# Loading and combining layer 0's weights differently at the start of a four-layer graph network kernel

## The chip, the cores and the metric

The kernel runs on one NeuronCore of a Trainium2 chip. A core has five engines, each with its own in-order queue: TensorE (PE; its weight loads are shown apart as PEld), VectorE (DVE), ScalarE (ACT), GpSimd (POOL) and SyncE (SP), which here only issues DMAs. ACT issues some DMAs too. All arithmetic is float32. The metric is the device time of one execution in microseconds (us); lower is better.

## The reference, cut to what matters

Four graph layers run one after another on x of 128 graphs x 128 nodes x 512 features. The change concerns layer 0 alone:

```python
Xw = X @ Wv + bv
sj = Xw @ aw[:d, 0]
si = Xw @ aw[d:, 0]
e = jax.nn.leaky_relu(sj[:, None, :] + si[:, :, None] + ab[0], negative_slope=0.2)
alpha_matrix = A * jnp.exp(e)
transition = alpha_matrix / (jnp.sum(alpha_matrix, axis=-1, keepdims=True) + 1e-12)
for k in range(Wk.shape[0]):          # K = 3
    H = H + Xk @ Wk[k] + bk[k]
    Xk = jnp.einsum('bij,bjd->bid', transition, Xk)
x = _layernorm(x + relu(H))
```

`Wv` is 512x512, `Wk` 3x512x512, `aw` 1024x1. The kernel never forms `Xw`: the scores need only the two vectors `Wv @ aw[:d]` and `Wv @ aw[d:]`, and it appends these as two more columns to the three `Wk` matrices.

## The kernel before

**Planner.** The kernel doesn't issue instructions as its Python runs. Each call on an engine is recorded in a `Plan` (line 173) with a due value (`plan.key`), an estimated cost and the tiles that it touches. `order` (238) then places all of them by list scheduling, on each engine the ready operation of the lowest due value or latest deadline first, takes tiles out of small pools (12 and later more buffers of kind `four`, 8 of `sq`, 6 PSUM banks and two more, `t0` and `t1`), and `emit` (364) issues them in that order. All instructions thus carry line 375 in the profile, and groups are told apart by their tiles. DMAs rotate through eight completion semaphores, called lanes here: a DMA is issued only when the DMA that last used its lane has landed, whichever of SP and ACT issued that.

**Products.** Every large product uses Strassen's scheme in Winograd's form, with seven block products in place of eight. In layer 0 it is applied twice (`twice`, 830, over `strassen`, 618): seven outer weights B11, B21, T2, T1, B22, T3, N4, and each of these holds seven inner blocks of 128 x 386 (three matrices' 128 columns each, and the two score columns). T1 = B12 - B11, T3 = B22 - B12, T2 = B22 - T1, N4 = B21 - T2. A 128x386 product is one matmul instruction and two records in the profile. The left operands are sums and differences of transposed x, made by POOL in `lefts` (793).

**Setup.** `prepare0` (882) makes the weights. `Wk` comes in four quarters: chunk pair g (0 or 1) by column half (0 or 1); a quarter and a matrix m is one `fetch` (898), four DMAs of 32 partitions each, 64 KB apiece. The two quarters of the left column half are issued from ACT (`fetch_quarter(ac, ...)`, 910 and 911), the two of the right half from SP (922, 923). They land in `stage`, three of the seven outer weight tiles (`first` in the profile). ACT copies each into place: twelve copies `first<-first 128x512`. Two `fetch` calls bring `Wv` (128 KB a DMA). `aw` is loaded broadcast over 128 partitions (`awb`), and eight `dot` calls (477) multiply rows of `Wv` with it and sum (DVE `junk<-four,four`), which gives the score columns. `combine` (503) makes the inner T3, T1, T2 and N4 of one quarter: three ACT copies into PSUM and four DVE subtractions. When B12 and B22 are there, `combine_once_more` (509) makes the outer weights: for each of seven inner blocks two ACT copies into `t0` and `t1` and two DVE subtractions (outer T1 and T2), and then two subtractions on POOL over whole tiles (`first<-first 128x2702`), outer T3 and N4. B12 is stored where T1 comes to lie.

**Two pairs of graphs.** `layer0` (967) takes four graphs at a time, transposes x (DVE `four<-four 128x1024`), makes the operands on POOL, runs the 49 block products, whose results DVE and ACT take out of the banks (`out<-bank`), and lets POOL add two `out` tiles (`out<-out 128x772`) after T1 and T3 (843 to 845). Then come attention, a round trip of the transition matrix through DRAM (`e`, `sq`), two more products into `t0` and `t1`, and the normalisation.

Of the kernel before, what the change touches and what calls it, by code (L numbers as in the profile page):

```python
# [14 lines left out]
OP = mybir.AluOpType  # L15
AX = mybir.AxisListType

P = 128
D = 512
C = D // P  # L20
# [34 lines left out]
B11, B21, T1, B22, T2, T3, N4 = range(7)  # L55
B12 = T1
# [9 lines left out]
QW = 3 * P + 2  # L66
# [311 lines left out]
def rows(ap, n):  # L378

    return bass.AP(tensor=ap.tensor, offset=ap.offset, ap=[[0, P], [1, n]])  # L380
# [3 lines left out]
def kernel(  # L384
# [20 lines left out]
    at = lambda kind, k: spans[kind][1] + k * SIZE[kind]  # L405
# [29 lines left out]
    for kind, k, t in (*(("out", k, t) for k, t in enumerate(outs)), ("w28", 0, places["w28"][0]),  # L435
                       ("row1", 0, row1)):
        for c in range(SIZE[kind] // SIZE["four"]):
            later["four", len(places["four"])] = [(kind, k)]
            places["four"].append(t[:, c * SIZE["four"]:(c + 1) * SIZE["four"]])
    plan = Plan(slots, later)  # L440
    pe, ve, ac, po, sp = (plan.engine(*e) for e in ((PE, nc.tensor), (DVE, nc.vector), (ACT, nc.scalar),
                                                     (POOL, nc.gpsimd), (SP, nc.sync)))

    def tile_of(kind, *shape, place=None):
        n = math.prod(shape)
        flat = View(Tile(kind, place=place), np.arange(SIZE[kind]))[:, :n]
        names = [f"a{k}" for k in range(len(shape))]
        return flat if len(shape) == 1 else flat.rearrange(
            f"p ({' '.join(names)}) -> p {' '.join(names)}", **dict(zip(names, shape)))

    def fixed(*shape, name, kind="fixed"):
        t = const.tile([P, *shape], FP, name=name)
        return View(Tile(kind, t), np.arange(math.prod(shape)).reshape(shape))

    def bank():
        return tile_of("bank", D)

    def four():

        return tile_of("four", U, D)  # L460
# [16 lines left out]
    def dot(dst, u, v, n=D):  # L477
        ve.scalar_tensor_tensor(junk[:, :n], u, 1.0, v, op0=OP.mult, op1=OP.mult, accum_out=dst)

    def row():  # L480
        return tile_of("row", D)
# [15 lines left out]
    def held_in_bank(kind, block):  # L497

        p = tile_of(kind, QW)
        ac.copy(p, block)  # L500
        return p

    def combine(W):

        c12, c22, c21 = (held_in_bank(k, W[:, j, 0]) for k, j in (("t0", B12), ("t1", B22), ("bank", B21)))
        for to, a, b in ((T3, c22, B12), (T1, c12, B11), (T2, c22, T1), (N4, c21, T2)):
            ve.tensor_tensor(W[:, to, 0], a, W[:, b, 0], OP.subtract)

    def combine_once_more(W):

        base = plan.key
        for n, i in enumerate((B11, T1, T2, B21, T3, B22, N4)):
            plan.key = base + .1 * n
            c12, c22 = (held_in_bank(k, W[j][:, i, 0]) for k, j in (("t0", B12), ("t1", B22)))
            for to, a, b in ((T1, c12, B11), (T2, c22, T1)):
                ve.tensor_tensor(W[to][:, i, 0], a, W[b][:, i, 0], OP.subtract)
        flat = [w.rearrange("p j o f -> p (j o f)") for w in W]
        for to, a, b in ((T3, T2, B11), (N4, B21, T2)):
            po.tensor_tensor(flat[to], flat[a], flat[b], OP.subtract)

    def prep():

# [358 lines left out]

    def prepare0():
        h = D // 2
        plan.key = -9.6
        awc, bvc = fixed(2 * C, name="aw_c"), fixed(C, name="bv_c")
        for c, v, n in ((awc, aw, 2 * C), (bvc, bv0, C)):
            sp.dma_start(c, bass.AP(tensor=v.tensor, offset=v.offset, ap=[[1, P], [P, n]]), run=1)
        ab_b, bk0b = fixed(1, name="ab_b"), row()
        sp.dma_start(bk0b[:3], bk0)
        sp.dma_start(ab_b, rows(ab, 1), run=1)  # L890
        plan.key = -9
        awb = four()
        sp.dma_start(awb.rearrange("p u f -> p (u f)"), rows(aw, 2 * D))
        W = WT["0"] = [tile_of("w7", 7, 1, QW, place=(B11, B21, T2, T1, B22, T3, N4).index(k)) for k in range(7)]
        stage = [W[T2 + m].rearrange("p j o f -> p (j o f)")[:, :C * D].rearrange("p (c f) -> p c f", f=D)
                 for m in range(3)]

        def fetch(queue, dst, src, chunks, columns, run):
            with plan.together():
                for k in range(4):  # L900
                    queue.dma_start(dst[k * Q:(k + 1) * Q],
                                    src.rearrange("(k c a) f -> k a c f", k=4, a=Q)[k][:, chunks, columns],
                                    run=run, parts=Q)

        def fetch_quarter(queue, g, half):
            for m in range(3):
                at = slice(2 * g, 2 * g + 2), slice(half * h, half * h + h)
                fetch(queue, stage[m][:, at[0], at[1]], wk0[m], *at, h)

        fetch_quarter(ac, 0, 0)  # L910
        fetch_quarter(ac, 1, 0)
        st = [four() for _ in range(2)]
        for g in range(2):
            fetch(sp, st[g], wv0, slice(2 * g, 2 * g + 2), slice(0, D), D)
        ones = fixed(P, name="ones")
        po.memset(ones, 1.0)
        two = fixed(C, 2, name="cols0")
        for c in range(C):
            for k in range(2):
                dot(two[:, c, k:k + 1], st[c // 2][:, c % 2], awb[:, k])  # L920
        plan.key = WHEN0[0] + .05
        fetch_quarter(sp, 0, 1)
        fetch_quarter(sp, 1, 1)
        plan.key = -9
        for g, half, j in ((0, 0, B11), (1, 0, B21), (0, 1, B12), (1, 1, B22)):
            for m in range(3):
                ac.copy(W[j][:, :4, :, m * P:(m + 1) * P].rearrange("p (n c) o i -> p c n (o i)", n=2),
                        stage[m].rearrange("p c (n i) -> p c n i", i=P)[:, 2 * g:2 * g + 2, 2 * half:2 * half + 2])
            scores = W[j][:, :4, 0, 3 * P:]
            if half:  # L930
                po.memset(scores, 0.0)
            else:
                po.memset(scores[:, 2:], 0.0)
                ac.copy(scores[:, :2], two[:, 2 * g:2 * g + 2])
            plan.key = COMBINE[half][g]
            combine(W[j])
            plan.key = -9
        plan.key = COMBINE[2]
        combine_once_more(W)
        plan.key = -9  # L940
        p = bank()
        aws = fixed(C, name="aw_sum")
        ve.tensor_add(aws, awc[:, :C], awc[:, C:])
        with plan.together(120):
            for j in range(C):
                pe.matmul(p[:, :1], aws[:, j:j + 1].to_broadcast([P, P]), bvc[:, j:j + 1],
                          start=j == 0, stop=j == C - 1)
        ve.tensor_tensor(c0, p[:, :1], ab_b, OP.add)

        p = bank()  # L950
        pe.matmul(p, ones[:3], bk0b[:3], start=True, stop=True)
        p = p.rearrange("p (h n i) -> p h n i", h=2, n=2)
        ac.copy(bias[:, 0], p[:, 0])
        ve.tensor_tensor(bias[:, 1], p[:, 1], bias[:, 0], OP.subtract)
        plan.key = WHENT[0][0] - .1
        for kind in ("t0", "t1"):
            p = tile_of(kind, D)
            pe.matmul(p, ones[:3], bk0b[:3], start=True, stop=True)
# [306 lines left out]
    h = D // 2  # L1265
# [246 lines left out]
    n = B // U  # L1512
# [18 lines left out]

    plan.key = -9
    prepare0()
    layer(layer0, 0, WHEN0, size=2)
    plan.late = LATE
# [38 lines left out]
```

## Time and profile before

| what | value |
|---|---|
| median of 3 runs | 5422.08 us (5418.66 to 5425.36) |
| the profiled execution | 5419.12 us, of which the span of the trace is 5417.3 us (1.8 us lie around it) |
| busy share of the span | PE 98%, PEld 78%, DVE 81%, ACT 44%, POOL 72% |
| mean granted TensorE clock | 0.998 |
| DMA | 814 MB, mean 150 GB/s |
| chain that ended last | PE 89%, DVE 4%, DMA 3%, waits for issue 2% |

Share by engine says what is busy on average. The chain that ended last follows the work back from the last instruction; a share of 89% for PE means that for most of the time an instruction on TensorE was what the end waited for. An engine's idle time in a stretch, and what is named as ending it, tells where that isn't so. Matmul ends are modelled, so a stretch in which PE reads as fully busy can hold idle time: in the first 10 us, for instance, PE reads 10.00 us busy with ten records, the last of which begins before 8 us.

### The profile page before, as it was taken

What the parts mean: (1) busy time and instruction counts of PE and PEld (TensorE: products, weight loads), DVE (VectorE), ACT (ScalarE), POOL (GpSimd) and SP (SyncE); (2) the same over time, 40 slices, a digit from 0 to 9 for tenths busy, and PEclk for the clock granted to TensorE, in tenths of its full rate; (3) what the DMA queues carried; (4) which work ended last, traced back from release to release, by engine and by line L of the source; (5) the groups of instructions that cost most, each with busy time, mean ns of one, the idle gap of its engine ahead of it and who ended that gap; (6) DMA issues with size and microseconds to landing.
All of it is one profiled execution on the core that took longest, in us unless ns stands there. A gap on an engine that the chain in (4) does not pass through costs nothing.

```text
span 5417.3 us, 93854 instructions
## 1 busy us (share of the span) xinstructions
PE 5318.2 (98%) x29035; PEld 4235.9 (78%) x29035; DVE 4411.2 (81%) x11725; ACT 2389.6 (44%) x6088; POOL 3907.2 (72%) x4931
## 2 busy tenths in 40 slices
PE   7999999999999999999999999999999999999998
PEld 3555555555788888888888888989988998999987
DVE  6778888887888888888888778778877877787886
ACT  3434334334444444444444444444444444444444
POOL 5777678765766666666767577778777777787776
PEclk9999999999999999999999999999999999999999
DMA  3444444445554545454545745545554555455543
GB/s 105 133 135 131 128 135 148 124 123 162 158 163 145 157 146 161 145 157 149 157 142 154 245 133 155 163 150 166 156 159 150 162 159 158 152 163 162 155 155 110
DMA packets 842748, 814.24 MB, mean 150 GB/s; under 512 B 269819, under 2 KB 643075, under 8 KB 842246
## 3 DMA queue, kind: packets, MB, share of 16 engines
q1 hardware_dynamic: 840326, 806.66, 48.5%
q8 instruction: 231, 3.78, 0.3%
q14 instruction: 271, 2.22, 0.1%
q10 hardware_dynamic: 1920, 1.57, 0.1%
HBM read 458.90 MB, written 349.04 MB: 149 GB/s over the span
## 4 chain that ended last, share of the span: by engine, by line
PE 89%; DVE 4%; DMA 3%; issue 2%; ACT 1%; SPq 1%; POOL 1%; ACTq 0%; DVEq 0%; POOLq 0%
PE bank L375 67%; PE t L375 21%; DVE out L375 1%; SPq L375 1%; DVE four L375 1%; DVE col L375 1%; DMA four<-in_x_dram 0%; ACT out L375 0%; DMA sq<-e 0%; DVE junk L375 0%; DMA first<-x3d 0%; DMA first<-in_L_gnn_Wk_dram 0%; ACT four L375 0%; POOL out L375 0%; DMA sq<-in_adj_dram 0%
## 5 line engine op out<-in xcount | busy, mean ns | idle before, releaser
L375 PE MATMUL bank<-first,four 128*128 128x386 f32 (+2 forms) x6008 | 1732.7, 432 | 38.0 <-DVE out L375 18.4
L375 PEld LDWEIGHTS bank<-first,four 128*128 128x128 f32 (+1 forms) x6008 | 1071.0, 189 | 610.5 <-DVE out L375 122.0
L375 DVE TENSOR_TENSOR out<-bank,out 128x386 f32<-128x386 f32 (+1 forms) x2089 | 1011.4, 501 | 262.2 <-PE bank L375 192.7
L375 DVE TENSOR_TENSOR four<-bank,four 128x256 f32<-128x256 f32 x1285 | 530.0, 418 | 206.8 <-PE bank L375 174.7
L375 POOL TENSOR_TENSOR col<-col,neghalf 128x2 f32<-128x2 f32 x320 | 233.7, 730 | 376.5 <-DVE col L375 374.4
L375 POOL TENSOR_TENSOR four<-four 128x256 f32<-128x256 f32 (+2 forms) x448 | 362.3, 821 | 181.4 <-DVE four L375 119.7
L375 POOL TENSOR_TENSOR out<-out 128x772 f32<-128x772 f32 (+3 forms) x233 | 327.6, 1414 | 216.5 <-DVE out L375 184.4
L375 PE MATMUL bank<-first,out 128*128 128x256 f32 (+1 forms) x1912 | 456.8, 374 | 10.8 <-DVE four L375 5.4
L375 POOL TENSOR_TENSOR four<-four,four 128x256 f32<-128x256 f32 (+2 forms) x501 | 436.0, 875 | 13.6 <-DVE four L375 3.8
L375 ACT COPY out<-bank 128x258 f32<-128x258 f32 (+2 forms) x523 | 208.1, 402 | 479.7 <-PE bank L375 410.2
L375 PEld LDWEIGHTS bank<-first,out 128*128 128x128 f32 (+1 forms) x1912 | 340.0, 187 | 77.3 <-DVE four L375 12.3
L375 ACT ACTIVATE four<-four,col,col 128x512 f32<-128x512 f32 (+1 forms) x300 | 263.7, 905 | 154.4 <-POOL col L375 147.2
L375 PE MATMUL bank<-four,first 128*128 128x256 f32 (+3 forms) x1680 | 304.0, 324 | 7.4 <-DVE out L375 2.5
L375 PE MATMUL t<-out,sq 128*128 128x512 f32 x512 | 260.1, 600 | 11.2 <-ACT t L375 5.6
L375 PE MATMUL bank<-out,first 128*128 128x128 f32 (+2 forms) x1636 | 269.3, 300 | 1.4 <-DVE out L375 1.1
L375 PEld LDWEIGHTS bank<-four,first 128*128 128x128 f32 (+2 forms) x1680 | 237.8, 182 | 35.7 <-DVE out L375 4.7
L375 ACT COPY t<-out 128x512 f32<-128x512 f32 x256 | 151.0, 591 | 229.4 <-DVE four L375 126.7
L375 ACT ACTIVATE out<-out,col,col 128x512 f32<-128x512 f32 (+1 forms) x191 | 166.6, 901 | 192.9 <-POOL col L375 192.8
L375 DVE BATCH_NORM_STATS2 col<-four 128x6 f32<-128x512 f32 x368 | 245.2, 681 | 5.8 <-ACT four L375 3.9
L375 DVE TENSOR_TENSOR four<-t,four 128x256 f32<-128x256 f32 x435 | 181.5, 418 | 81.0 <-PE t L375 72.5
L375 PEld LDWEIGHTS bank<-out,first 128*128 128x128 f32 (+1 forms) x1636 | 224.9, 187 | 20.7 <-issue 2.3
L375 PE MATMUL t<-first,four 128*128 128x256 f32 (+1 forms) x902 | 232.7, 377 | 0.0
(533 smaller groups left out, 13054.6 us busy)
## 6 DMA issues: line engine op xcount, KB each, us to landing
four<-h SPq DMA_DIRECT2D x72, 512.0 KB, 4.8
h<-four SPq DMA_DIRECT2D x272, 128.0 KB, 2.5
four<-in_x_dram SPq DMA_DIRECT2D x504, 64.0 KB, 2.0
four<-in_x_dram SPq DMA_DIRECT2D x61, 512.0 KB, 4.2
x1d<-four SPq DMA_DIRECT2D x61, 512.0 KB, 2.9
four<-x1d SPq DMA_DIRECT2D x61, 512.0 KB, 4.0
out<-x1d SPq DMA_DIRECT2D x54, 512.0 KB, 5.2
first<-S SPq DMA_DIRECT2D x54, 512.0 KB, 4.2
```

The source lines that it names most:

```text
L375: call(*map(real, args), **{n: real(a) for n, a in kw.items()})
```

## The change

- `aw` is loaded once as one row of 4 KB into one partition. Two matmuls of `ones` (one partition, 128 columns) with its halves spread it over 128 partitions into two PSUM banks, and the eight dots read it there.
- The small vectors (`aw` and `bv` by columns, `bk`, `ab`) are issued as one group from ACT, and stand first in its queue; before, SP issued them, `ab` only at 34.81 us.
- Of the left half's second quarter (g = 1) matrix 0 is loaded from ACT, matrices 1 and 2 from SP; before, all three came from ACT.
- The right half comes in three fetches over all four chunks, 12 DMAs of 128 KB, in place of 24 of 64 KB.
- The inner differences of quarter B12 are made by POOL alone (`combine_apart`): four subtractions of 128x386 from SBUF to SBUF, no copies into PSUM.
- Outer T3 and N4 are made in two pieces each: inner blocks 0 to 3 (128x1544), then 4 to 6 (128x1158).

```diff
+    def combine_apart(W):
+
+        for to, a, b in ((T3, B22, B12), (T1, B12, B11), (T2, B22, T1), (N4, B21, T2)):
+            po.tensor_tensor(W[:, to, 0], W[:, a, 0], W[:, b, 0], OP.subtract)
+
     def combine(W):
...
         for to, a, b in ((T3, T2, B11), (N4, B21, T2)):
-            po.tensor_tensor(flat[to], flat[a], flat[b], OP.subtract)
+            for at in (slice(0, 4 * QW), slice(4 * QW, 7 * QW)):
+                po.tensor_tensor(flat[to][:, at], flat[a][:, at], flat[b][:, at], OP.subtract)
...
-        plan.key = -9.6
-        awc, bvc = fixed(2 * C, name="aw_c"), fixed(C, name="bv_c")
-        for c, v, n in ((awc, aw, 2 * C), (bvc, bv0, C)):
-            sp.dma_start(c, bass.AP(tensor=v.tensor, offset=v.offset, ap=[[1, P], [P, n]]), run=1)
-        ab_b, bk0b = fixed(1, name="ab_b"), row()
-        sp.dma_start(bk0b[:3], bk0)
-        sp.dma_start(ab_b, rows(ab, 1), run=1)
-        plan.key = -9
-        awb = four()
-        sp.dma_start(awb.rearrange("p u f -> p (u f)"), rows(aw, 2 * D))
+        plan.key = -9.7
+        awr = four().rearrange("p u f -> p (u f)")
+        sp.dma_start(awr[:1], aw.rearrange("f o -> o f"), run=2 * D, parts=1)
...
-        def fetch_quarter(queue, g, half):
-            for m in range(3):
-                at = slice(2 * g, 2 * g + 2), slice(half * h, half * h + h)
-                fetch(queue, stage[m][:, at[0], at[1]], wk0[m], *at, h)
-
-        fetch_quarter(ac, 0, 0)
-        fetch_quarter(ac, 1, 0)
+        def fetch_part(queue, m, chunks, half):
+            at = chunks, slice(half * h, half * h + h)
+            fetch(queue, stage[m][:, at[0], at[1]], wk0[m], *at, h)
+
+        low, high, every = slice(0, 2), slice(2, 4), slice(0, 4)
         st = [four() for _ in range(2)]
-        for g in range(2):
-            fetch(sp, st[g], wv0, slice(2 * g, 2 * g + 2), slice(0, D), D)
+        for g, chunks in enumerate((low, high)):
+            plan.key = -9.7 + .2 * g
+            fetch(sp, st[g], wv0, chunks, slice(0, D), D)
+        plan.key = -9
+        for m in range(3):
+            fetch_part(ac, m, low, 0)
+        awc, bvc = fixed(2 * C, name="aw_c"), fixed(C, name="bv_c")
+        ab_b, bk0b = fixed(1, name="ab_b"), row()
+        with plan.together():
+            for c, v, n in ((awc, aw, 2 * C), (bvc, bv0, C)):
+                ac.dma_start(c, bass.AP(tensor=v.tensor, offset=v.offset, ap=[[1, P], [P, n]]), run=1)
+            ac.dma_start(bk0b[:3], bk0, parts=3)
+            ac.dma_start(ab_b, rows(ab, 1), run=1)
+        for m in range(3):
+            fetch_part(sp if m else ac, m, high, 0)
...
+        awb = [bank() for _ in range(2)]
+        for k in range(2):
+            pe.matmul(awb[k], ones[:1], awr[:1, k * D:(k + 1) * D], start=True, stop=True)
         two = fixed(C, 2, name="cols0")
         for c in range(C):
             for k in range(2):
-                dot(two[:, c, k:k + 1], st[c // 2][:, c % 2], awb[:, k])
+                dot(two[:, c, k:k + 1], st[c // 2][:, c % 2], awb[k])
         plan.key = WHEN0[0] + .05
-        fetch_quarter(sp, 0, 1)
-        fetch_quarter(sp, 1, 1)
+        for m in range(3):
+            fetch_part(sp, m, every, 1)
...
-            combine(W[j])
+            (combine_apart if j in (B12,) else combine)(W[j])
```

Because a planner sets the order, the diff alone doesn't tell what moves. Set side by side, the two built programs issue the same operations in the same order, but for buffer numbers, from the 71st of 14694 TensorE instructions on (the 73rd of the changed one), from SP's 109th of 4388, POOL's 78th of 4936, ACT's 112th of 5090 and DVE's 334th of 11191. Everything that differs lies ahead of these. In the head of the changed program the queues stand so:

- SP: `aw` row, first half of `Wv` (4), x (8), second quarter matrices 1 and 2 (8), second half of `Wv` (4), the right half (12), x (8, then more), where before it was small vectors, `aw` broadcast, `Wv` (4), x (8), `Wv` (4), x (8), the right half (24), `ab`, x.
- ACT: small vectors (4), first quarter (12), table load, copy, second quarter matrix 0 (4), copies.
- POOL: operands of the first pair (4), `combine_apart` (4), operands of the second pair (13), T3 and N4 first pieces, `sq` scaling and `out` sums with the second piece of T3 between them, the last operand of S4 (`four` 128x256), two 128-wide operands with N4's second piece between them, then the next pair.

## Prediction

> **What bounds the kernel now.** I read the page's slices first, to see where TensorE isn't full.
>
> ```profile
> PE   7999999999999999999999999999999999999998
> PEclk9999999999999999999999999999999999999999
> ```
>
> Only the first slice (135 us) falls short, and the clock is full throughout. As both programs issue the same order from the 71st TensorE instruction on, the change can pay only in that slice. Next I read the busy time by stretches of 10 us (columns: PE, PEld, DVE, ACT, POOL, clock, DMA share, GB/s).
>
> ```profile
> 0.00:10.00 10.00, 3.84 (x10) 2.28 (x10) 0.16 (x1) 0.00 (x0) 1.06 (x13) 1.00 0.66 139
> 10.00:20.00 10.00, 0.00 (x0) 0.00 (x0) 4.29 (x10) 3.60 (x6) 0.89 (x2) 1.00 0.77 216
> 20.00:30.00 10.00, 6.22 (x8) 2.17 (x8) 7.45 (x18) 6.45 (x15) 2.37 (x4) 1.00 0.48 141
> 30.00:40.00 10.00, 1.73 (x3) 1.15 (x4) 5.21 (x12) 5.79 (x12) 10.00 (x13) 1.00 0.47 134
> ...
> 60.00:70.00 10.00, 7.40 (x23) 4.02 (x23) 5.08 (x11) 0.46 (x2) 10.00 (x5) 1.00 0.00 0
> ```
>
> TensorE stands nearly idle to 20 us and again from 30 to 40, with a dent from 60 to 70 where POOL is full. The timeline names the waits (start, length, instruction, count, idle time before and its releaser).
>
> ```profile
> 11.18 1.28 ACT L375 ACT_TABLE_LOAD   x1 [11.18 <-DMA first<-in_L_gnn_Wk_dram]
> ...
> 19.26 0.62 ACT L375 COPY first<-first 128x512 f32<-128x512 f32 x1 [1.64 <-DMA first<-in_L_gnn_Wk_dram]
> ...
> 20.16 1.66 PE L375 MATMUL bank<-first,four 128*128 128x386 f32 x2 [11.79 <-ACT first L375]
> ...
> 23.53 11.23 SPq L375 DMA_DIRECT2D first<-in_L_gnn_Wk_dram  x24
> ...
> 36.36 0.62 ACT L375 COPY first<-first 128x512 f32<-128x512 f32 x1 [1.27 <-DMA first<-in_L_gnn_Wk_dram]
> 37.43 0.37 ACT L375 COPY out<-bank 128x258 f32<-128x258 f32 x1
> 38.27 7.06 PE L375 MATMUL bank<-first,four 128*128 128x386 f32 x13 [9.49 <-DVE out L375]
> ```
>
> The first product waits for ACT, whose copies stand behind its own DMA issues. The second gap ends when a bank is emptied, and that `out<-bank` copy stands on ACT behind the copies of the right half, which SP issues one per 0.47 us, 24 times, to 34.8 us. The last part:
>
> ```profile
> 54.87 0.55 DVE L375 TENSOR_TENSOR first<-t,first 128x386 f32<-128x386 f32 x1
> 55.50 10.84 POOL L375 TENSOR_TENSOR first<-first 128x2702 f32<-128x2702 f32 x2 [13.77 <-DVE first L375]
> 66.30 3.58 POOL L375 TENSOR_TENSOR out<-out 128x772 f32<-128x772 f32 x2
> 68.75 8.70 PE L375 MATMUL bank<-first,four 128*128 128x386 f32 x26 [2.60 <-DVE out L375]
> ```
>
> DVE ends the outer differences at 55.4, POOL makes outer T3 and N4 in 10.84 us, its `out` sum stands behind them, and TensorE waits for it until 68.75. After that it doesn't stop for long.
>
> **What the Trainium skill says.** "PSUM — Partial Sum Buffer", section "Engine vs sequencer instructions": the queues of ScalarE, VectorE and GpSimd are strictly first in, first out, and matmuls start in program order. The trace agrees: the 0.37 us copy at 37.43 and the sum at 66.30 come right after what stood ahead of them. "DMA: Bandwidth & Descriptors", "Issuing engines are not separate DMA queues": DMAs of all issuers share the same 16 engines, and a second issuer saves issue time only. Here two issuers reached 216 GB/s between 10 and 20 us, SP alone with 64 KB loads 141 and 134 after it. "GPSIMD Engine Reference", "Engine selection": elementwise work with two inputs costs about twice VectorE's, and GpSimd has no access to PSUM. For 128x256 the trace has 0.73 us on POOL and 0.42 on DVE.
>
> **The change part by part.** I follow the after queues to the first matmul behind the 68.75 stall, and compare there.
>
> *Loads.* `aw` falls from 512 KB (6.9 us to landing, the longest) to 4 KB. Before, the right half's last copy began at 36.36, after 1.05 MB of Wv, 3.15 of Wk, 1.05 of x and 0.52 of `aw`. In the changed queues it lies behind 4.7 MB: Wv, Wk and one pair's x (0.52). The first 10 us stay slow (lanes held by the 4-byte-element vectors, 3.3 us to landing, four issues of 0.42 to 0.58 us now ahead on ACT): 1.39 MB as before. The other 3.3 MB at the 216 GB/s of the mixed stretch take 15.4 us: landed at 25.4. Bounds: at the best slice of the head (277 GB/s) 22; or the 1.57 MB of the right half start at 17.5 (SP's earlier 25 DMAs, by lane waits of 2.5 to 3.4 us) and run at the old 139 GB/s plus 2 us landing: 30.8. I take 25.4, since a 128 KB load per 0.47 us issue no longer lets issue be the limit.
>
> *First product.* ACT has 8 DMAs fewer between its first copies (second quarter), where the issues of 12.71 to 19.2 stood. I put the first product at 15 to 16, not 20.16. This is not added: the right half's landing overtakes it.
>
> *Spreading `aw`.* Two matmuls of about 1 us each (the `bank<-row,ones` pair took 2.07) on an idle TensorE: nothing. The dots read PSUM: 0.69 us each before; between -0.1 and +0.1 each by DVE's 128x386 operations from PSUM (0.55), so 0 taken, at most 0.8 in eight. The second four wait for Wv's second half (about 19 to 21) and hold two banks until then; that's ahead of the right half, so hidden. If Wv came after 25 it would be bare.
>
> *B12 on POOL.* Three ACT copies (0.48) and four DVE subtractions (0.55) go; four POOL operations of 386 columns, between 0.73 (256) and 1.27 (512), so 1.0 each, 4.0 in all. They wait for B12's last copy (25.4 + 0.6 = 26.0), end at 30.0, and thirteen operand operations of the second pair queue behind them. These wait for the transposed x on DVE anyway, at 25.4 + two copies 1.2 + a `t` copy 0.5 + DVE's four operations and the transpose (3.4) = 30.6. So hidden by 0.6 us; if the transpose comes earlier, POOL is late instead, by up to 4.
>
> *Outer differences.* From the first to the last DVE has 30 operations: 29 at 0.49 (27 took 13.2 us before) + 1.24 = 15.4, from 27.6 to 43.0; before they ended at 55.4. What T3's first piece needs (six of the seven blocks) is there at 41.5.
>
> *POOL.* The thirteen operands: four 512 wide at 1.24, seven 256 wide at 0.69, two 128 wide at 0.41 = 10.6; 30.6 + 10.6 = 41.2. So POOL and DVE meet at 41.5. Then the first pieces, 5.42 x 1544/2702 = 3.10 each, 6.2; two `sq` scalings at 0.59, 1.2; two `out` sums at 1.79, 3.6; T3's second piece 2.32: 13.3, to 54.8. The `four` operand that S4's products need now stands behind all this: +0.7 = 55.5. The pieces add two instructions, some 0.2 us in POOL's spacing; what they save is that the sums no longer stand behind 10.84 us. This operand is what is late next: TensorE stops at its 45th instruction row until 55.5.
>
> *The rest of the head.* Before, from 68.75 to 87.30 there are 26 rows to the common tail, 18.55 us. The changed order has 26 of the same mix from that operand on: 55.5 + 18.55 = 74.05. The gain is 87.30 - 74.05 = 13.2. I take off 0.7 for handovers of ACT, DVE and PE in the shortened stretch (about 0.05 to 0.1 each in the chain): 12.5. Against the profiled execution 5419.1 - 12.5 = 5406.6. That execution lies 3.0 below the median of the runs shown; on the median's footing the forecast is 5409.6, a gain of 0.23%. About 0.2%, 10.8 us, is what a measurement of this kernel can tell from no change.
>
> **The rivals.**
>
> *Transfers no faster (R2).* The DMA engines, not the issue, give the 139 GB/s. For: the second half of the DMA page's words, and 0.77 DMA share at 216 GB/s leaves little. Against: 277 and 216 were reached with smaller loads. The landing is then 30.8, 5.4 later, the chain behind it shifts by as much: gain 7, 5415.
>
> *More than counted (R3).* Landing near 22, and the S4 operand found by TensorE without a stop: the chain moves 3 to 4 us more. Gain 16, 5406. For: DVE was busy only half of 30 to 40. Against: POOL's 24 us of queued work.
>
> *Slower (R4).* Lanes: SP's loads wait for lanes of ACT's loads; ACT issues its last four only after a copy that waits for loads, and SP stood 7.1 us before a Wk load already. Now SP carries 8 more loads behind such lanes. If that makes the right half land late, POOL's subtractions, operands and pieces all follow, us for us. It decides from 25.4 + 13 = 38.4 on; at 42 it costs 3.6: 5426. Against it: ACT's blocking part has shrunk from 12 loads to 4. A real loss of 10.8 needs landing at 49, for which nothing speaks.
>
> **How the numbers follow.** Likeliest case 0.62, R2 0.20, R3 0.11, R4 0.07. The likeliest case's own range is 5407 to 5413 (gain 9 to 15). R2 and R3 with their bounds and 3 us of scatter between runs give 5402 to 5418, which leaves R4 and the tails out. Faster by over 0.2%: three quarters of the likeliest (0.47) and R3 (0.11), 0.58; slower by over 0.2%: the far end of R4 and what I don't see, 0.05; within: 0.37.
>
> **What would show it.** First product at 15 to 16; 12 loads of 128 KB issued by 25; the last `first<-first 128x512` copy on ACT at about 26; `first<-first 128x386` on POOL from 26 to 30; `128x1544` from 41.5; a TensorE stop ending at about 55.5 with POOL `four` as its releaser; the second 10 us of PE no longer empty, and the stretch from 30 to 40 fuller. Wrong if the last copy comes after 31 (R2, R4), if TensorE stops again between 74 and 130 where POOL has the extra 4 us, or if anything beyond 150 us takes a different time.

## The result, and the profile after

| what | before | after |
|---|---|---|
| median (7 runs each, side by side) | 5418.68 us (5411.58 to 5425.36) | 5401.65 us (5395.73 to 5407.13) |
| ratio, with its 95% interval | | 0.9969 (0.9957 to 0.9981) |
| the profiled execution; its span | 5419.12; 5417.3 us | 5406.97; 5405.0 us |

The kernel is faster by 0.31%, and the interval lies wholly beyond no change. A second set of runs of the same two kernels (the experiment `again`) gave 0.9972. The forecast of 5409.6 us lies 8 us too high, and the 5401.65 lie just below the range that went with it, 5402 to 5418.

The slices on the page of after: the first one has risen from 7 to 8 tenths.

```profile
PE   8999999999999999999999999999999999999998
PEclk9999999999999999999999999999999999999999
```

The busy time by stretches of 10 us of after (columns as before: PE, PEld, DVE, ACT, POOL, clock, DMA share, GB/s):

```profile
0.00:10.00 10.00, 7.54 (x14) 3.44 (x14) 1.45 (x4) 0.33 (x1) 1.06 (x13) 1.00 0.60 137
10.00:20.00 10.00, 2.91 (x4) 1.17 (x4) 5.17 (x13) 7.59 (x15) 2.83 (x4) 1.00 0.68 183
20.00:30.00 10.00, 4.71 (x7) 1.86 (x8) 6.17 (x17) 4.05 (x10) 0.02 (x1) 1.00 1.11 206
30.00:40.00 10.00, 8.66 (x18) 4.08 (x18) 7.53 (x16) 3.97 (x9) 6.78 (x7) 1.00 0.54 149
40.00:50.00 10.00, 8.53 (x23) 3.30 (x22) 9.90 (x26) 6.53 (x18) 10.00 (x12) 1.00 0.13 36
50.00:60.00 10.00, 10.00 (x25) 5.31 (x25) 6.90 (x14) 0.93 (x3) 8.55 (x6) 0.83 0.14 36
60.00:70.00 10.00, 10.00 (x31) 5.62 (x30) 7.36 (x15) 2.43 (x5) 10.00 (x10) 1.00 0.41 112
```

From 30 to 40 us TensorE is now mostly busy (8.66 us instead of 1.73), and the dent from 60 to 70 is gone (10.00 instead of 7.40). New is a clock of 0.83 from 50 to 60. The timeline of after has the waits (start, length, instruction, count, idle time before and its releaser):

```profile
15.99 2.91 PE L375 MATMUL bank<-first,four 128*128 128x386 f32 x4 [6.19 <-DVE four L375]
...
18.43 5.65 SPq L375 DMA_DIRECT2D first<-in_L_gnn_Wk_dram  x12
...
21.11 0.69 DVE L375 SCALAR_TENSOR_TENSOR junk<-four,bank 128x512 f32<-128x512 f32 x1 [2.77 <-DMA four<-in_L_gnn_Wv_dram]
...
23.61 1.63 PE L375 MATMUL bank<-first,four 128*128 128x386 f32 x2 [4.72 <-DVE out L375]
...
29.01 0.37 ACT L375 COPY out<-bank 128x258 f32<-128x258 f32 x1 [1.57 <-PE bank L375]
29.28 1.14 ACT L375 COPY first<-first 128x512 f32<-128x512 f32 x2
...
29.98 3.85 POOL L375 TENSOR_TENSOR first<-first 128x386 f32<-128x386 f32 x4 [11.14 <-ACT first L375]
...
35.50 1.23 DVE L375 STREAM_TRANSPOSE four<-four 128x1024 f32<-128x1024 f32 x1
36.81 1.27 POOL L375 TENSOR_TENSOR four<-four 128x512 f32<-128x512 f32 x1 [2.99 <-DVE four L375]
...
47.36 6.34 POOL L375 TENSOR_TENSOR first<-first 128x1544 f32<-128x1544 f32 x2
...
51.08 17.52 PE L375 MATMUL bank<-first,four 128*128 128x386 f32 x48
```

The first product comes 4.2 us earlier and the right half's loads are issued by 24.1 us instead of 34.8. But a new wait stands at 21.11: the dots of Wv's second half wait for a load, and an `out` sum that TensorE needs is behind three of them in VectorE's queue. The last copies of the right half (29.28) no longer wait for a load. GpSimd's first outer pieces begin at 47.36, where the undivided operation began at 55.50. The last line is the other part of the gain: 48 matmul records run without an idle time in between, where TensorE stopped for 2.60 us before.

Followed instruction by instruction, after leads before by 9.6 us at 100 us, 8.4 at 225, 11.4 at 250, 11.1 at 350, 13.0 at 1400 and 12.9 at 5350. So the head gives about nine, a step near 245 us three, and the rest little. The step lies far beyond the head, where both programs issue the same order; it is split below, under what was not expected.

### The profile page after: what moved, and what is told of

The parts are those of the page before. It is cut to its first block, busy times and chain, and to the rows that moved or that the text cites. A ratio compares the mean times of both kernels' runs of the same rounds, so it can differ in the third digit from the quotient of the medians.

```text
span 5405.0 us, 93824 instructions
## 1 busy us (share of the span) xinstructions
PE 5324.9 (99%) x29039; PEld 4239.3 (78%) x29039; DVE 4410.1 (82%) x11721; ACT 2387.5 (44%) x6085; POOL 3913.6 (72%) x4937
## 4 chain that ended last, share of the span: by engine, by line
PE 87%; DVE 5%; DMA 3%; issue 1%; SPq 1%; ACT 1%; POOL 1%; ACTq 0%; DVEq 0%; POOLq 0%
PE bank L375 66%; PE t L375 21%; DVE out L375 1%; SPq L375 1%; DVE col L375 1%; DVE four L375 1%; DMA first<-x3d 1%; DMA four<-in_x_dram 1%; ACT out L375 0%; DMA out<-x3d 0%; DMA sq<-e 0%; POOL out L375 0%; DVE junk L375 0%; DVE first L375 0%; DMA sq<-in_adj_dram 0%
## 5 line engine op out<-in xcount | busy, mean ns | idle before, releaser
L375 PE MATMUL bank<-first,four 128*128 128x386 f32 (+2 forms) x6008 | 1735.6, 433 | 27.3 <-DVE out L375 11.4
L375 PE MATMUL bank<-first,out 128*128 128x256 f32 (+1 forms) x1912 | 458.6, 375 | 10.4 <-DVE four L375 6.2
L375 DVE BATCH_NORM_STATS2 col<-four 128x6 f32<-128x512 f32 x368 | 244.7, 679 | 4.1 <-ACT four L375 1.7
```

Of the source, the lines that this page charges most:

```text
L375: call(*map(real, args), **{n: real(a) for n, a in kw.items()})
```

## The experiments

The part of the program up to about 200 us is planned anew for every edit, so that each kernel below has its own order there, and the same one beyond. "After" and "the changed kernel" are the same thing below. An edit therefore shows a part of the change together with what the planner makes of it. One shift recurs: in loads_only, no_apart, small_loads, aw_broadcast and wv_first SP issues the second pair's x ahead of the right half, whose last load then lands at 30.3 to 33.0 us, not at 27.7 as in after. No run holds that order fixed. Two questions were open: which part brings the gain, and what the wait at 21.11 costs. Beside the runs below the kernel before had a median of 5413.77 us (39 runs; again, before_again, loads_only, compute_only), 5415.21 (41; whole, no_apart, small_loads, wv_first) and 5416.56 (27; wv_right, aw_broadcast, big_only). An interval of a ratio here is 0.0006 to 0.0013 wide to each side, 3 to 7 us.

**Repeats: again and before_again.** The changed kernel and the kernel before, with no edit.

> The changed kernel once more. Theory A: all of the gain is made in the first 100 us (9.5 us in the trace) and in one dip of the TensorE clock that falls into the head in place of 245 us (about 2 us), and the 17 us between the two medians is 12 plus scatter. Then this run is 10 to 14 us faster than before, and its trace lies within 1 us of the first trace's times at 100 us. Theory B: something later in the program gains another 4 to 5 us each time (other buffers, other collisions of DMAs). Then it is 16 to 18 us faster, and against a second trace of the kernel before the lead at 5400 us is 14 or more.

> The kernel before once more, for its trace. Theory A: it lies within 2 us of the first trace everywhere between 100 and 5400 us, apart from dips of the clock, and the lead of the changed kernel is 9 to 11 us at 150 us and 11 to 13 at the end. Theory B: the lead at the end is 14 or more while it is 9 to 11 at 150 us. Time against itself: within 3 us of nothing.

Measured: again 5400.89 us (5392.9 to 5405.8), ratio 0.9972 (0.9963 to 0.9981); before_again 5415.26, ratio 1.0002 (0.9994 to 1.001). In the traces again leads before by 12.5 us at 100 us, 14.9 at 250, and 17.7 at the end. Its head is 2.9 us shorter than that of after with the same program: the dots get Wv at 20.23 instead of 21.11, and the first outer pieces begin at 44.45 instead of 47.36. So one execution of the head scatters by three microseconds, where theory A allowed one. Whether the extra beyond 250 us is real (theory B) is not settled: it is 1.5 and 2.8 us in these two pairs with before, and the two traces of the kernel before themselves drift apart by 2 us there.

**Parts alone: loads_only and compute_only.** The loads, the small vectors and the spread `aw` without the two edits on GpSimd; and those two edits on the kernel before.

```diff
 loads_only, against the changed kernel
-            for at in (slice(0, 4 * QW), slice(4 * QW, 7 * QW)):
-                po.tensor_tensor(flat[to][:, at], flat[a][:, at], flat[b][:, at], OP.subtract)
+            po.tensor_tensor(flat[to], flat[a], flat[b], OP.subtract)
...
-            (combine_apart if j in (B12,) else combine)(W[j])
+            combine(W[j])
```

> The loads and the spreading of aw changed, B12 combined by ACT and DVE and outer T3 and N4 whole, as in the kernel before. Theory A (loads earlier and less queueing on ACT are the gain, POOL's two parts hide or cost nothing): 7 to 11 us faster. Rival C (POOL's two parts carry half of it, since the last stop of TensorE before was behind the undivided 10.84 us): 3 to 6 us faster, with a stop of TensorE of 2 us or more behind a 128x2702 operation.

> Loads and aw as in the kernel before; B12's differences on POOL and outer T3 and N4 in two pieces each. Theory A: 0 to 3 us faster (the 2.6 us stop at 68.75 goes, the gaps to 20 us and from 29 to 38 stay). Rival C: 6 us or more faster.

Measured: loads_only 5411.85 us, ratio 0.9996 (0.9988 to 1.0004); compute_only 5413.15, 0.9995 (0.9987 to 1.0004). Neither can be told from no change. Taken at their middles they are worth 2.2 and 2.7 us (0.0004 and 0.0005 of 5414), 4.9 together and uncertain by about 6, where the whole change is worth 15 to 17. So the parts, each as the planner placed it, do not add up. The timeline of loads_only has why:

```profile
44.03 5.12 PE L375 MATMUL bank<-first,four 128*128 128x386 f32 x8 [4.89 <-DVE first L375]
...
52.65 10.83 POOL L375 TENSOR_TENSOR first<-first 128x2702 f32<-128x2702 f32 x2 [5.81 <-DVE first L375]
...
65.89 15.43 PE L375 MATMUL bank<-first,four 128*128 128x386 f32 x38 [3.65 <-DVE out L375]
```

Counted by matmul records, this kernel leads before by 10.1 us at 38.7 us. Then TensorE stops for VectorE (4.89), and again behind the undivided operation (3.65), and at 90 us only 0.9 of the lead is left. In compute_only it is the other way round: its right half still lands at about 35.5, the first piece on GpSimd starts at 55.03, only 0.5 us earlier than before, and little but the shorter stop behind it (1.36 instead of 2.60) is gained:

```profile
55.03 6.34 POOL L375 TENSOR_TENSOR first<-first 128x1544 f32<-128x1544 f32 x2 [9.70 <-DVE first L375]
...
67.57 7.40 PE L375 MATMUL bank<-first,four 128*128 128x386 f32 x22 [1.36 <-DVE out L375]
```

The sizes that theory A gave for loads_only (7 to 11) were wrong, rival C's stops were right; for compute_only the middle lies in theory A's range, and the interval (up to 7 us) just reaches rival C's 6.

**One part taken out: whole, no_apart, small_loads, aw_broadcast.**

```diff
 whole
-            for at in (slice(0, 4 * QW), slice(4 * QW, 7 * QW)):
-                po.tensor_tensor(flat[to][:, at], flat[a][:, at], flat[b][:, at], OP.subtract)
+            po.tensor_tensor(flat[to], flat[a], flat[b], OP.subtract)
 no_apart
-            (combine_apart if j in (B12,) else combine)(W[j])
+            combine(W[j])
 small_loads
-        for m in range(3):
-            fetch_part(sp, m, every, 1)
+        for g in (low, high):
+            for m in range(3):
+                fetch_part(sp, m, g, 1)
 aw_broadcast
-        sp.dma_start(awr[:1], aw.rearrange("f o -> o f"), run=2 * D, parts=1)
+        sp.dma_start(awr.rearrange("p u f -> p (u f)"), rows(aw, 2 * D))
...
-            pe.matmul(awb[k], ones[:1], awr[:1, k * D:(k + 1) * D], start=True, stop=True)
...
-                dot(two[:, c, k:k + 1], st[c // 2][:, c % 2], awb[k])
+                dot(two[:, c, k:k + 1], st[c // 2][:, c % 2], awr[:, k])
```

> The changed kernel with outer T3 and N4 of the first pair again as single 128x2702 operations on GpSimd; the rest as changed. Theory A (the head needs all three parts, and each lost one costs a TensorE stop): GpSimd can start T3 only when VectorE's last outer difference is done, at about 48.6 us, and is full for 10.8 us, to 59.4; the 128x772 out sum (at 55.74 in the changed kernel) stands behind it, so TensorE stops for 2 to 5 us at about 55 to 62, and the kernel is 2 to 6 us slower than the changed one (5403 to 5407, if the changed one is at 5401). Rival D (dividing is worth nothing; the loads need only the differences on GpSimd): no stop, within 1.5 us of the changed kernel.

> The changed kernel with B12's differences again by ScalarE copies and VectorE subtractions; the two outer operations stay divided. Theory A: four more VectorE operations of 0.55 us before the outer differences and three ScalarE copies; VectorE, which has no idle time from 36.7 to 51 us in the changed kernel, ends 2 to 2.5 us later and the start of the first 128x1544 piece and TensorE's full stretch with it: 2 to 5 us slower than the changed kernel. Rival D (these differences carry nearly all of what the parts give together): 8 to 11 us slower, as slow as loads_only was. Rival E (GpSimd doing them is a loss there, since its operands wait behind them): up to 3 us faster than the changed kernel.

> The changed kernel with the right half of layer 0's projections in 24 loads of 64 KB instead of 12 of 128 KB; the rest as changed. Theory A: 24 issues at 0.47 us from 18.4 end at 29.7, the last copy comes at about 31 to 32 instead of 29.3 (where it no longer waits for a load but for its turn), so GpSimd's differences and all behind them are 1.5 to 3 us later: 1 to 3 us slower than the changed kernel. Rival G (the size of the loads is the larger part of the gain): 5 us slower or more.

> The changed kernel with the attention vector loaded to all 128 partitions (512 KB) again, not spread by TensorE; the rest as changed. Theory A (every part of the head stands in the way when it alone is as before): 0.5 MB more at about 200 GB/s, 2.5 us, stands ahead of Wv, x and the right half; the first product moves from 15.99 to 17.5 to 19.5 and TensorE's full stretch by 1 to 3 us: 1 to 4 us slower than the changed kernel. Rival H (the vector's load is the head of all waits: each part undone so far cost 5 to 10): 6 us slower or more. Rival I (the stretch hides it): within 1 us.

Measured: whole 5405.98 us, ratio 0.9983 (0.9976 to 0.9989); no_apart 5408.63, 0.9990 (0.9982 to 0.9998); small_loads 5411.13, 0.9993 (0.9985 to 1.0001); aw_broadcast 5404.02, 0.9978 (0.9970 to 0.9986). Against the 0.9972 of again that is a loss of about 6, 10, 11 and 3 us. Each such difference of two ratios is uncertain by about 6 us, so only the losses of no_apart and small_loads are clear of none. The middles for whole and aw_broadcast lie in theory A's ranges; for whole the stop in its trace speaks as well, for aw_broadcast rival I (no loss) isn't excluded. For no_apart and small_loads the middles lie above A's losses and in the ranges of rivals D and G; for no_apart A's upper end is still within the uncertainty. In the profiled executions, though, no_apart's lead over before (10.4 us at 250 us) is only 1.0 and 4.5 short of the two of the changed kernel, so its size rests on the medians alone. The timeline of whole shows the stop that dividing removes:

```profile
45.76 10.85 POOL L375 TENSOR_TENSOR first<-first 128x2702 f32<-128x2702 f32 x2 [0.15 <-DVE first L375]
56.56 1.81 POOL L375 TENSOR_TENSOR out<-out 128x772 f32<-128x772 f32 x1
...
59.03 10.39 PE L375 MATMUL bank<-first,four 128*128 128x386 f32 x26 [3.44 <-DVE out L375]
```

The `out` sum stands behind 10.85 us of GpSimd, and TensorE waits 3.44 us for what follows from it. The timelines of no_apart (first two lines) and of small_loads:

```profile
42.28 5.12 PE L375 MATMUL bank<-first,four 128*128 128x386 f32 x8 [4.89 <-DVE first L375]
...
49.50 6.34 POOL L375 TENSOR_TENSOR first<-first 128x1544 f32<-128x1544 f32 x2 [4.39 <-DVE first L375]
```

```profile
21.95 11.42 SPq L375 DMA_DIRECT2D first<-in_L_gnn_Wk_dram  x24
...
52.57 6.34 POOL L375 TENSOR_TENSOR first<-first 128x1544 f32<-128x1544 f32 x2 [2.28 <-DVE first L375]
...
65.11 7.40 PE L375 MATMUL bank<-first,four 128*128 128x386 f32 x22 [1.54 <-DVE out L375]
```

In no_apart VectorE is what is late: TensorE waits for it, and GpSimd stands idle for 4.39 us before its first piece. In small_loads the twenty-four issues end at 33.4 us, and the first piece begins 5 us later than in after. Part of that, how much isn't shown, is the planner's: here and in no_apart SP issues the second pair's x ahead of the right half.

**The large loads alone: big_only.** The kernel before with nothing but the right half in twelve loads.

```diff
-        fetch_quarter(sp, 0, 1)
-        fetch_quarter(sp, 1, 1)
+        for m in range(3):
+            fetch(sp, stage[m][:, :, h:], wk0[m], slice(0, 4), slice(h, 2 * h), h)
```

> The kernel before with only the right half of layer 0's projections in 12 loads of 128 KB instead of 24 of 64 KB. Theory A: issue ends at about 29.5 instead of 34.76 and the last copy comes at about 31.5 instead of 36.4, but VectorE's outer differences and the 10.84 us of undivided GpSimd operation behind them take back most of it: 0 to 4 us faster than the kernel before. Rival G (the size of the loads alone carries what small_loads lost): 8 us faster or more.

Measured: 5413.69 us, ratio 0.9997 (0.9988 to 1.0005). Theory A held, rival G fell: the edit whose removal costs about 11 us brings about 1.6, and at most 6.5, when the rest is as before. GpSimd's 128x2702 starts at 55.10 there, 0.4 us earlier than before, since VectorE is full (10.00 us from 40 to 50) in front of it, and TensorE stops behind it for longer than before:

```profile
55.10 10.83 POOL L375 TENSOR_TENSOR first<-first 128x2702 f32<-128x2702 f32 x2
...
68.34 16.70 PE L375 MATMUL bank<-first,four 128*128 128x386 f32 x46 [3.94 <-DVE out L375]
```

**The wait at 21.11: wv_first and wv_right.** Both halves of Wv next to each other, so that the dots need not wait; in the first the planner put the right half 4.8 us later than in after (issued from 23.2), in the second that is undone.

```diff
 both
-        for g, chunks in enumerate((low, high)):
-            plan.key = -9.7 + .2 * g
-            fetch(sp, st[g], wv0, chunks, slice(0, D), D)
+        with plan.together():
+            for g, chunks in enumerate((low, high)):
+                for k in range(4):
+                    sp.dma_start(st[g][k * Q:(k + 1) * Q],
+                                 wv0.rearrange("(k c a) f -> k a c f", k=4, a=Q)[k][:, chunks, :], run=D, parts=Q)
 wv_right only
-        plan.key = WHEN0[0] + .05
+        plan.key = -9.2
```

> The changed kernel with both halves of layer 0's Wv loaded next to each other right after the attention vector, so that the second half doesn't stand behind the second pair's x and lands at about 15 instead of 21.0. Theory A (the wait for that half holds VectorE's queue, and with it TensorE's second stretch, ScalarE's last copies and GpSimd's B12 differences): the dots are done by 19, the matmuls at 23.61 move to 19 to 20, the GpSimd differences from 29.98 to 25 to 27, TensorE's full stretch from 44.2 to 39 to 41: 3 to 6 us faster than the changed kernel. Rival F (the transposed x and the operand operations of GpSimd set the full stretch, and with x later in the queue they come no earlier): within 1.5 us of the changed kernel.

> The changed kernel with both halves of layer 0's Wv loaded next to each other after the attention vector, and the right half of its projections directly behind the second quarter, as in the changed kernel (wv_first had the second pair's x ahead of it, and its twelve loads 5.5 us later). So only the place of Wv's second half is moved. Theory A: the dots are done by about 17, TensorE's second stretch starts at 20 to 21.5 instead of 23.61 (22.73 in its repeat), the last ScalarE copy of the right half is set by its landing, at 25 to 27, GpSimd's B12 differences start at 26 to 28, and TensorE's full stretch at 39 to 41.5 instead of 44.2 (42.1): 2 to 5 us faster than the changed kernel, ratio to the kernel before 0.996 to 0.9966. Rival F (the second pair's transposed x and its 10.6 us of GpSimd operands set the full stretch, whatever the dots do): the full stretch starts at 42 to 44.5, within 1.5 us of the changed kernel.

Measured: wv_first 5398.86 us (5393.3 to 5399.95, 5 runs), ratio 0.9966 (0.9954 to 0.9979); wv_right 5398.71 (5395.21 to 5400.35, 5 runs), 0.9968 (0.9956 to 0.9981). Neither ratio can be told from 0.9969 and 0.9972 of the changed kernel. The timeline of wv_right:

```profile
13.45 0.69 DVE L375 SCALAR_TENSOR_TENSOR junk<-four,bank 128x512 f32<-128x512 f32 x1 [1.89 <-DMA first<-in_L_gnn_Wk_dram]
...
18.89 2.91 PE L375 MATMUL bank<-first,four 128*128 128x386 f32 x4 [8.91 <-DVE four L375]
...
29.32 1.14 ACT L375 COPY first<-first 128x512 f32<-128x512 f32 x2 [0.64 <-DMA first<-in_L_gnn_Wk_dram]
30.02 3.84 POOL L375 TENSOR_TENSOR first<-first 128x386 f32<-128x386 f32 x4 [8.28 <-ACT first L375]
...
46.09 6.33 POOL L375 TENSOR_TENSOR first<-first 128x1544 f32<-128x1544 f32 x2 [0.31 <-DVE first L375]
```

The dots are done by 16.3, as theory A said. But the last copies start at 29.32 as in after (29.28), and now they wait for the load again; the first product has moved back to 18.89, as x came later. The right half's last load lands at 28.5, where it landed at 27.7 in after and 26.9 in again: the edit takes the wait away and moves the landing back with it, so the cost of the wait alone isn't shown. By the traces theory A's times fell for both: the B12 differences begin at 33.2 and 30.0, not by 28, and TensorE's full stretch at 45.0 and 44.5, not by 41.5. The times alone can't tell A from rival F, whose stretch (42 to 44.5) wv_right just meets.

**What joins them.** TensorE has a fixed amount of work in the head, and is not full until the outer weights come. Two times account for most of the differences: when GpSimd begins the first outer operation of the pair, and for how long TensorE stops behind it. The sum is (55.50 - begin) + (2.60 - stop), from the two values of before.

| kernel | begin, us | stop, us | sum, us | lead over before at 250 us | ratio |
|---|---|---|---|---|---|
| big_only | 55.10 | 3.94 | -0.9 | 0.8 | 0.9997 |
| compute_only | 55.03 | 1.36 | 1.7 | 2.9 | 0.9995 |
| loads_only | 52.65 | 3.65 | 1.8 | 4.1 | 0.9996 |
| small_loads | 52.57 | 1.54 | 4.0 | 5.4 | 0.9993 |
| no_apart | 49.50 | none | 8.6 | 10.4 | 0.9990 |
| whole | 45.76 | 3.44 | 8.9 | 10.5 | 0.9983 |
| aw_broadcast | 46.88 | 0.28 | 10.9 | 10.4 | 0.9978 |
| after | 47.36 | none | 10.7 | 11.4 | 0.9969 |
| wv_right | 46.09 | none | 12.0 | 14.6 | 0.9968 |
| wv_first | 46.33 | 1.66 | 10.1 | 13.2 | 0.9966 |
| again | 44.45 | none | 13.7 | 14.9 | 0.9972 |

The lead follows the sum within -0.5 to +3.1 us. It is taken behind the step near 245 us, which brings every one of these kernels 1.6 to 3.2 us against before; at 225 us, ahead of it, the lead follows the sum within -2.3 to +0.1 us (8.4 for after, 12.3 for again, -2.2 for big_only). The stop needs the pieces, as whole shows. What the begin needs is less plain. In after the first piece follows the thirteenth operand of the second pair without idle time, and these thirteen wait for the transposition at 35.50, late in VectorE's queue. In aw_broadcast and wv_first the right half landed at 32.2 and 32.0, over 4 us later than in after, and the piece still began at 46.88 and 46.33: GpSimd stood idle 2.98 and 3.44 us before it, so it was ready for an earlier start. So landing ahead of 32 doesn't bring the begin forward by itself; what VectorE and GpSimd still have to do behind it counts as well. That the B12 differences on GpSimd free VectorE for this fits no_apart and loads_only, whose begins are late behind VectorE, but there the landing was later too (30.8 and 30.3).

## Why the prediction was right or wrong

*The likeliest case.* "Against the profiled execution 5419.1 - 12.5 = 5406.6": the profiled execution of after took 5406.97, and both ratio intervals (gains of 10 to 23 and 10 to 20 us) hold 12.5. Sign and main mechanism, an earlier and fuller head, are right. That the size for this pair is right too is partly luck: the head gave 9.3 us by its tail and 8.4 at 225 us, not 13.2, and most of the rest came from the step near 245 us, which the prediction did not have; "anything beyond 150 us takes a different time" was one of its own signs of being wrong. More than half of that step is a dip of the clock. "The clock is full throughout" was read from slices of 135 us, whose 9 says no more than 90% or above; the trace of before has the clock at half from 244.9 to 248.3 us.

*The step that put the time wrong* is "on the median's footing the forecast is 5409.6", with "3 us of scatter between runs" for the range. It took a median of three runs as a footing good to less than three microseconds. With four more runs the same kernel measured 5418.68, and in the later sets 5413.77, 5415.21 and 5416.56, none as high as the 5422.08 used. Of the miss of 7.95 us, 3.4 is the footing (5422.08 - 5418.68), 4.5 the gain of the medians (17.0 instead of 12.5). Either alone would have left the time inside the range (5406.2 with the first, 5405.1 with the second); together they put it just below. The profiled pair shows less than the medians because the profiled execution of after is the second slowest of its seven, 5.3 us above their median, and that of before lies only 0.4 above the median of its own seven. The interval doesn't separate 17.0 from the forecast's 12.5: the spans of the four pairs of profiled executions differ by 12.3, 14.1, 18.0 and 19.8 us. Whether the true gain is nearer to 12 or to 17 stays open.

*Inside the head two terms were mis-sized, in opposite directions.*

- "Loads": landed at 25.4. The issue was as said (12 in 5.65 us), the rate was not: 137, 183 and 206 GB/s in the three stretches, not 216 in the last two. By 20 us 3.2 MB have come (1.37 + 1.83); the 1.5 MB left of 4.7 at 206 GB/s take 7.3 us: 27.3. The trace has the last recorded landing at 27.7. The 216 GB/s came from a stretch with two issuers. "The Trainium skill", in "DMA: Bandwidth & Descriptors", section "Issuing engines are not separate DMA queues", says that all issuers share the same 16 engines, which allows carrying it over; in after SP alone, issuing from 20 to 30 us, reached 206. R2's 139 GB/s was wrong as well: 64 KB per issue of 0.47 us is 139 GB/s, so that was the pace of the issue. Nor does a share of 0.77 "leave little", as R2 had it: before has 374 GB/s at a share of 1.16 from 242 to 244 us.
- "B12 on POOL" and "Outer differences" follow from it: 26.0 became 29.98, 27.6 to 43.0 became 33.01 to 48.6. The length was right (15.6 instead of 15.4), the beginning 5.4 late: 2.3 from the landing, the rest from ScalarE's and VectorE's queues, where copies and transpositions stand behind bank emptying. That the chain behind the landing "shifts by as much" is not borne out: aw_broadcast, where x was issued ahead of it, landed 4.5 us later than after, and its first piece began 0.5 us earlier. "The transpose by 30.6" came at 36.7, as it lay behind eight other operations of VectorE from 29.4 us on.
- "POOL": 10.6 us for thirteen operands was 10.55; the first piece 3.17 (3.10 said), B12's four 3.85 (4.0 said). It began at 47.36 instead of 41.5, and the S4 operand was ready at about 63 instead of 55.5.
- "This operand is what is late next: TensorE stops at its 45th instruction row until 55.5" is the term that took this back. There is no such stop, though the operand came 8 us later than said. In the changed order the 45th row needs T3's second piece, ready at 60.8 when TensorE gets there at 61.3, and the operand serves a row 2.6 us later still. TensorE was then simply full, from 44.2 us on. This was R3's "found by TensorE without a stop", while R3's landing near 22 did not come.
- "The rest of the head": the tail was reached at 77.97, not at 74.05, so the gain there is 9.3 us and not 13.2; of the 3.9 us that are short, the clock took about 1.7 (below).

*Spreading aw costs nothing.* Right: the dots from PSUM took 0.69 us each, as from SBUF. Its being "hidden" in Wv's second half was wrong (VectorE waited 2.77 us at 21.11); what that cost isn't shown, as wv_right, without the wait, has the same time and a later landing.

*First product.* 15.99, inside 15 to 16. *R4* did not come: no load waited long enough.

## What to carry to other kernels

Where three engines hand work on in a chain, price a change by what each handover needs together: an edit whose removal cost about 11 us was worth about 1.6 alone, though a planner that moves other loads with it is part of both numbers. Take a stop in a prediction only after finding which instruction of the new order really needs the late tile, and check it against TensorE's amount of work up to there. Look for what lies beyond the changed stretch too: a quarter of this pair's gain came from a step where both programs issue the same order. For a gain of 0.2% to 0.3%, the reference time itself wants more than three runs; forecast the ratio or the pair of profiled executions first, and give the absolute time the scatter of the medians.

## What was not expected of the hardware

**The granted TensorE clock falls to half for 3.4 us or a multiple of it, and when it does so changes with the program.** Stretches of 2 us of after, and then of before (columns as above):

```profile
50.00:52.00 2.00, 2.00 (x5) 0.93 (x5) 2.00 (x4) 0.18 (x1) 2.00 (x2) 0.85 0.00 0
52.00:54.00 2.00, 2.00 (x4) 1.01 (x3) 0.51 (x3) 0.38 (x1) 2.00 (x2) 0.50 0.00 0
54.00:56.00 2.00, 2.00 (x6) 1.10 (x5) 1.32 (x3) 0.00 (x0) 0.56 (x2) 0.80 0.10 16
```

```profile
242.00:244.00 2.00, 0.32 (x1) 0.00 (x0) 1.33 (x4) 0.21 (x1) 2.00 (x3) 1.00 1.16 374
244.00:246.00 2.00, 1.29 (x2) 0.66 (x3) 2.00 (x5) 1.17 (x3) 1.92 (x3) 0.73 0.96 292
246.00:248.00 2.00, 2.00 (x4) 0.98 (x3) 0.42 (x2) 1.18 (x2) 0.82 (x2) 0.50 1.02 350
```

In the dip matmul records start every 0.64 us instead of every 0.32. The trace of before has it at 244.9 to 248.3 us and its repeat at 244.7 to 248.1, and neither has one between 44 us and there; after has it at 51.4 to 54.8, again at 48.6 to 52.1, and none of the eleven traces of other kernels has it at 245. Each costs 1.7 us (half of 3.41), so after pays it in the head and gets it back at 245. The lead goes there from 8.44 to 9.70 at the wait for a `t` copy (2.39 us before, 1.13 after) and to 11.40 in the dip; between the repeats from 12.64 to 12.95 and to 14.64.

At its start the trace has more of it than the clock column tells. The first clock record, a rise to full, comes at 43.5 us in before, 34.3 in after and 28.2 in again; ahead of it there is none, so the 1.00 of the column is no reading there. Up to it the first products of after (15.99, four records in 2.91 us) also start 0.64 us apart, and so do 17 records up to 33.8 us; in again only 10 do, up to 27.2 us. At 0.32 us each that is 2.2 us, which may be part of the 2.9 us between the two heads. "The Trainium skill", in "TensorE: Matmul & The Clock Gate", section "What's actually happening", says that the array runs at half its clock after an idle window of about 3.4 us and at full clock after as long a busy one. The first products agree with it (6.19 us of idle time ahead of them). The dip at 51 us looks as if it didn't: TensorE reads as busy from 44.2 us on.

What sets its moment can be worked out from the traces. In each of the thirteen, all changes of the clock lie on a grid of 3.41 us. Take the matmul records with a left operand of 128 rows in each stretch of that grid, priced at full clock (0.32 us for 386 columns, other widths in proportion). All 62 falls to half follow a stretch where these come to less than 1.4 us, and no stretch at full clock where they come to less than 1.27 us kept it. TensorE ahead of the two falls, in after (three lines) and in before:

```profile
48.13 1.12 PE L375 MATMUL t<-row,ones 3*128 3x512 f32 x2
49.19 0.92 PE L375 MATMUL bank<-first,four 128*128 128x386 f32 x2
50.03 1.12 PE L375 MATMUL t<-row,ones 3*128 3x512 f32 x2
```

```profile
244.71 1.90 PE L375 MATMUL t<-out,sq 128*128 128x512 f32 x2 [2.39 <-ACT t L375]
```

In after the stretch from 48.0 to 51.4 holds seven records, but four of them are `t<-row,ones` with a left operand of three rows, and the other three come to 1.0 us. In before the stretch from 241.5 to 244.9 holds the 2.39 us wait, and 0.9 us of such records. So the window need not be idle, and the products with three rows do not seem to fill it; this is read off the traces, no run was made for it.

**Loads of 128 KB moved more at the same pace of issue.** From 20 to 30 us of after, when most of the bytes were the twelve loads of 128 KB, 206 GB/s came at a DMA share of 1.11; the same ten microseconds of before, with loads of 64 KB at the same 0.47 us an issue, had 141 GB/s at 0.48. The share doesn't tell that the engines were full, as before has 374 GB/s at 1.16 above. One issue of 128 KB per 0.47 us would allow 279 GB/s (an estimate from these two numbers), so the issue did not hold them at 206; what did stays open.
